# Reordering the opening and the change of sweep of a two-sweep graph kernel, spreading the first rows with TensorE, loading each weight block once, and computing one more product from fp32r words

## The chip, the cores and the metric

The kernel runs on one core of one Trainium2 chip. The metric is the device time of one execution in microseconds, the median of several runs. Repeats of one kernel spread by 1 to 9.5 us, up to 0.34%, and the profiled execution can be any of them, so a difference of a few us between two profiles proves nothing by itself.

## The reference

64 samples, each of 256 tokens with 768 features. Each is layer-normalised and rectified, and three matrices are applied: to the neighbours' mean (`adj`), to the reverse neighbours' mean, and to the token itself. Terms of rank one (biases, degrees, relation embeddings) and the input are added.

```python
h = jnp.maximum(_layernorm(x), 0.0)                       # (64, 256, 768)
ctx = jnp.matmul(adj, h @ Wadj.T + badj) / deg_c[..., None]
ctx = ctx + jnp.matmul(radj, h @ Wrev.T + brev) / rdeg_c[..., None]
ctx = ctx + h @ Wself.T + bself
rel = agg @ Wr.T + br * deg[..., None] + ragg @ Wrr.T + brr * rdeg[..., None]
return x + ctx + rel
```

## The kernel before

For each sample the aggregated features form a left matrix of two token halves (a, b) by three kinds (0, 1, 2). The weights form a right matrix of three kinds by three blocks of 256 columns, so nine blocks of 768 x 256. The kernel replaces 18 block products by 15 products of sums, listed with the right-hand sums they need:

```python
PRODUCTS = {
    6: ("a0+a2+b2", "+01 -20"),
    12: ("a0+a2+b0+b2", "-01"),
    1: ("b0", "-00 +10 +01"),
    # ... (12 more)
}
```

The 15 weight sums are not all held at once: there are two sweeps over the 64 samples. Sweep one makes the left matrices and does eight products, then stores left matrices and partial sums to DRAM. Sweep two reads them back and does the other seven (7, 9, 15, 6, 4, 12, 1).

A product is six matmuls of 128x128 by 128x256. As plain float32 that is 12 records. A product is summed up in a *bank*, an accumulator in PSUM that the listings call x, y, z and so on. Some products are instead made of **words**: both operands are split into a rounded fp32r part and two scaled differences, and three groups of six fp32r matmuls replace the plain ones. The first two groups must come first in their bank, because the bank is then rescaled as a whole (condensed):

```python
def split_left(b, n):
    nc.scalar.activation(first, value, AF.Copy, scale=LOWER)
    top = top_copy(b, n, first.bitcast(F32))              # ScalarE, into the one PSUM tile "top"
    nc.vector.tensor_tensor(others, value, top, op=ALU.subtract)
    nc.vector.scalar_tensor_tensor(diff, others, -STEP, top, op0=ALU.mult, op1=ALU.add)

def product_first(b, n, bank):                            # 12 word matmuls, start=True, then
    nc.scalar.activation(bank, bank, AF.Copy, scale=1.0 + 1.0 / STEP)

def add_out(b, bank, sign, c, n, many=1):                 # DVE: o (+/-)= bank
```

Everything is scheduled by hand: strings such as `STEP2` name the steps in program order, and each engine works through its own instructions in that order; in the traces below an addition on DVE that was ready at about 1695 us ran at 1707.55, behind three sums that stand before it. A quote mark means "the next sample", a caret a sample of sweep two named while sweep one still runs (`load^` sample 0, `load^^` sample 1), a number alone a product, `W`/`V` loads a weight block, `w`/`v` combines blocks in place, `s` splits a left operand, `5a` is the first part of product 5 in words, `u` aggregates, `o`/`out` load and store partial sums. The change of sweep began by loading left operands from ScalarE's queue (condensed):

```python
def change_sweep():
    first_sweep.close()
    second["pool"] = main.enter_context(tc.tile_pool(name="second", bufs=1))
    load_left(0); load_sums(0, 0, 2); load_left(1)
STEP2 = "7a a0+a2+b0+b2 a1+a2' b1+b2' a0+a2' 9 s4 15a 7 6 load'' s9' 15 4a tokT 12 s7' o0' 4 out0 s15' 9a' a0+a2+b2' 1 out1 o1'"
```

## Time and profile before

| | before |
|---|---|
| median of 3 runs | 2839.2 us |
| TensorE busy | 2736.3 us, 96% |
| period in sweep one / sweep two | 25.53 / 16.60 us a sample |
| last sample of sweep one starts | 1716.67 us |
| TensorE idle, 0 to 250 us | 73 us |

The page gives totals; the busy time by stretch shows where TensorE is not full; the timeline shows starts and lengths of single groups. TensorE's instructions overlap, so lengths are read from start to start. The lines are in the prediction below.

For the bookkeeping I use two markers that exist in all kernels: the start of product 10 of the last sample in sweep one, and the start of product 7 of the last sample in sweep two.

### The profile page before, as it was taken

What the parts mean: (1) busy time and instruction counts of PE and PEld (TensorE: products, weight loads), DVE (VectorE), ACT (ScalarE), POOL (GpSimd) and SP (SyncE); (2) the same over time, 40 slices, a digit from 0 to 9 for tenths busy, and PEclk for the clock granted to TensorE, in tenths of its full rate; (3) what the DMA queues carried; (4) which work ended last, traced back from release to release, by engine and by line L of the source; (5) the groups of instructions that cost most, each with busy time, mean ns of one, the idle gap of its engine ahead of it and who ended that gap; (6) DMA issues with size and microseconds to landing.
All of it is one profiled execution on the core that took longest, in us unless ns stands there. A gap on an engine that the chain in (4) does not pass through costs nothing.

```text
span 2837.7 us, 43467 instructions
## 1 busy us (share of the span) xinstructions
PE 2736.3 (96%) x16112; PEld 2488.7 (88%) x16112; DVE 1817.8 (64%) x2892; ACT 1498.4 (53%) x2734; POOL 1864.6 (66%) x1289
## 2 busy tenths in 40 slices
PE   4789999999999999999999997999999999999999
PEld 3578988898888888888888986899999999999998
DVE  4566666666666666666666664666666666666665
ACT  3356565655666565655666552444444444444443
POOL 4477777777777777777777775555555555555553
PEclk8899999999999999999999998999999999999999
DMA  8367777777777777777777767566666666666664
GB/s 268 130 231 264 251 260 272 258 257 257 262 270 257 253 259 273 258 258 254 262 271 257 252 239 270 196 251 236 238 246 247 232 240 252 238 237 244 251 236 159
DMA packets 240353, 698.48 MB, mean 246 GB/s; under 512 B 19444, under 2 KB 100852, under 8 KB 223752
## 3 DMA queue, kind: packets, MB, share of 16 engines
q1 hardware_dynamic: 203272, 393.64, 40.9%
q10 hardware_dynamic: 36864, 302.01, 28.1%
q8 instruction: 129, 2.11, 0.3%
q14 instruction: 88, 0.72, 0.1%
HBM read 439.46 MB, written 256.11 MB: 245 GB/s over the span
## 4 chain that ended last, share of the span: by engine, by line
PE 93%; DVE 3%; DMA 2%; ACT 1%; issue 0%; POOL 0%; ACTq 0%; SPq 0%; DVEq 0%; POOLq 0%
PE y L530 19%; PE x L530 19%; PE pa L496 12%; PE z L530 7%; PE w L530 7%; PE u L519 3%; PE v L519 3%; PE t L519 3%; PE x L519 3%; PE w L519 3%; PE y L519 3%; PE z L519 3%; PE u L530 2%; PE v L530 2%; PE t L530 2%; DVE w L258 1%
## 5 line engine op out<-in xcount | busy, mean ns | idle before, releaser
L513 POOL TENSOR_TENSOR X<-X,Xs 128x768 f32<-128x768 f32 x256 | 472.1, 1866 | 493.7 <-DVE l L293 217.8
L530 PE MATMUL y<-w,X 128*128 128x256 f32 x2304 | 536.4, 383 | 18.9 <-POOL X L513 9.2
L530 PEld LDWEIGHTS y<-w,X 128*128 128x128 f32 x2304 | 432.2, 192 | 80.1 <-POOL X L513 9.5
L485 POOL TENSOR_TENSOR xT<-xT,row 128x1536 f32<-128x1536 f32 (+1 forms) x128 | 447.3, 3494 | 70.9 <-DMA row<-d 65.9
L496 PE MATMUL pa<-a,hilo 128*128 128x512 f32 x1536 | 416.1, 399 | 33.5 <-DVE hilo L452 18.2
L501 DVE TENSOR_TENSOR X<-pa,row 128x512 f32<-128x512 f32 x384 | 264.0, 689 | 183.5 <-PE pa L496 175.4
L530 PE MATMUL x<-w,X 128*128 128x256 f32 x1548 | 356.8, 380 | 8.0 <-DVE o L543 8.0
L277 ACT ACTIVATE top<-l 128x768 f32<-128x768 f32 x350 | 285.3, 815 | 145.9 <-DVE l L294 47.3
L496 PEld LDWEIGHTS pa<-a,hilo 128*128 128x128 f32 x1536 | 271.0, 191 | 80.6 <-DVE hilo L452 22.8
L294 DVE SCALAR_TENSOR_TENSOR l<-l,top 128x768 fp32r<-128x768 f32 x350 | 333.8, 954 | 12.0
L530 PEld LDWEIGHTS x<-w,X 128*128 128x128 f32 x1548 | 285.6, 191 | 42.7 <-issue 8.3
L513 POOL TENSOR_TENSOR b2-a<-Xs,X 128x768 f32<-128x768 f32 x64 | 116.0, 1812 | 196.2 <-ACT hilo L446 162.4
L452 DVE SCALAR_TENSOR_TENSOR hilo<-x,cols,top_h 128x768 fp32r<-128x768 f32 x128 | 129.9, 1015 | 163.6 <-ACT top_h L277 163.6
L293 DVE TENSOR_TENSOR l<-X,top 128x768 fp32r<-128x768 f32 x186 | 176.5, 949 | 11.8 <-ACT top L277 11.4
L530 PE MATMUL z<-w,Xs 128*128 128x256 f32 x768 | 177.9, 382 | 0.0
L530 PE MATMUL w<-w,a1+b 128*128 128x256 f32 x768 | 176.4, 379 | 0.0
L530 PE MATMUL x<-w,Xs 128*128 128x256 f32 x768 | 176.2, 379 | 0.0
L291 ACT ACTIVATE l<-X 128x768 fp32r<-128x768 f32 x186 | 155.6, 836 | 22.4 <-issue 19.9
L530 PEld LDWEIGHTS z<-w,Xs 128*128 128x128 f32 x768 | 142.7, 192 | 18.9
L530 PEld LDWEIGHTS w<-w,a1+b 128*128 128x128 f32 x768 | 141.3, 190 | 18.6
L530 PEld LDWEIGHTS x<-w,Xs 128*128 128x128 f32 x768 | 141.0, 190 | 17.1 <-DVE o L543 0.4
L545 DVE TENSOR_TENSOR o<-o,y 128x256 f32<-128x256 f32 x128 | 53.5, 418 | 156.7 <-PE y L535 156.7
(182 smaller groups left out, 5567.9 us busy)
## 6 DMA issues: line engine op xcount, KB each, us to landing
kept_X<-X ACTq DMA_DIRECT2D x64, 1536.0 KB
X<-kept_X ACTq DMA_DIRECT2D x64, 1536.0 KB
o<-in_x_dram SPq DMA_DIRECT2D x128, 384.0 KB
xT<-in_x_t_dram SPq DMA_DIRECT2D x64, 768.0 KB
kept_Xs<-Xs ACTq DMA_DIRECT2D x64, 768.0 KB
sums<-o SPq DMA_DIRECT2D x128, 384.0 KB
Xs<-kept_Xs ACTq DMA_DIRECT2D x64, 768.0 KB
o<-sums SPq DMA_DIRECT2D x128, 384.0 KB
```

The source lines that it names most:

```text
L277: nc.scalar.activation(top.rearrange("p (f i) -> p f i", i=of.shape[-1]), of, AF.Copy)
L291: nc.scalar.activation(first, value, AF.Copy, scale=LOWER)
L293: nc.vector.tensor_tensor(others, value, top, op=ALU.subtract)
L294: nc.vector.scalar_tensor_tensor(diff, others.bitcast(F32), -STEP, top, op0=ALU.mult, op1=ALU.add)
L452: nc.vector.scalar_tensor_tensor(hilo[:, 1, c, :], S[b]["x"][:, c, :], rstd, top, op0=ALU.mult, op1=ALU.subtract)
L485: eng.tensor_tensor(v, v, row[:, k : k + 1, :].to_broadcast([P, f1 - f0, L]), op=op)
L496: nc.tensor.matmul(pa, hilo[:, part, c, ts(f, P)], s["a"][:, c, :, :].rearrange("p s i -> p (s i)"), start=(k == 0), stop=(k == 2 * C - 1),)
L501: nc.vector.tensor_mul(s["X"][:, f, :, :].rearrange("p s i -> p (s i)"), pa, s["row"][:, 2:4, :].rearrange("p s i -> p (s i)"))
L513: (eng or nc.gpsimd).tensor_tensor(L[name], L[x], L[y], op=op)
L519: nc.tensor.matmul(bank, l[k][:, f, :], r[k][:, f, :], start=(k == 0 and f == 0), stop=(k == 1 and f == F - 1))
L530: nc.tensor.matmul(bank, l[:, f, :], r[:, f, :], start=(start and f == 0), stop=(row is None and f == F - 1), skip_group_check=not start,)
L545: nc.vector.tensor_sub(o, o, bank)
```

## The change

The intent was to fill TensorE's holes in the opening and between the sweeps, and to take some of its cycles away in sweep two. The core of the diff, with cuts marked:

```diff
-    "12": (12, "x", 4, ((-1, 1, 1),)),
-    "1": (1, "x", 5, ((-1, 1, 0),)),
+    "12": (12, "x", 4, ((-1, 1, 0, 2),)),
+    "1a": (1, "s", None, None),
+    "1": (1, "s", 5, ((-1, 1, 0),)),
 ...
 FIRST = """
-o0 o1 adj xt W10 degrees0 degrees1 statistics0 statistics1 tokens spread adj' x' W"11" W5 rows1 ...
+o1 o0 statistics0 adj degrees0 statistics1 xt degrees1 x' W10 tokens W02 left normalise0 normalise1
+statistics0' W12 spread row1 row0 W20 adj' second1 rows1 W11 degrees0' second0 self0 u5 u4 self1 u3 u0 W22 ...
 SECOND = """
-o1' 10a left' self0' self1' degrees0'' degrees1'' u0' 5a 10 statistics0'' statistics1'' tokens'' u1' 5 8 ...
+u2' 5a x'' b2-a1 degrees0'' o0 o1' degrees1'' a1+b1 b0+b1 u5' self0' self1' u3' 10a a1+b0+b1 a0+a1+b0+b1 5
+statistics0'' 10 statistics1'' u1' 8 11a tokens'' 11 ...
 LAST1 = """
-10a sweep2 5a 10 5 V7 V9 V15 s11 V6 V4 V12 flag a0+a2^ a1+a2^ ... v1 out0
+sweep2 10a a0+a1+b0+b1 10 a2+b2 5a V11 5 flag V21 8 load^ v15 s11 14 13 V20 V00 11a v4 V01 11 V10 o0^ b1+b2^
+2 a1+a2^ load^^ a0+a2^ v6 out0 v1 V22 3 out1 a0+a2+b2^ v9 v7 v12
 FIRST2 = """
+o1 a0+a2' 9 6 s9' load'' a0+a2+b0+b2 a1+a2' 4 tokT 7 12 1 out0 a1+a2'' o0' 15 o1' s7' 9a' out1 a0+a2''
 STEP2 = """
+b1+b2' 7a 9 s4 15a a1+a2' a0+a2' a0+a2+b2' 7 load'' s1 4a 15 a0+a2+b0+b2 6 tokT s9' o0' 1a 4 s7' 12 out0 o1'
+1 s15' out1 9a'
-IN_WORDS = {5: 2, 10: 3, 11: 4, 9: 1, 7: 1, 15: 2, 4: 2}
+IN_WORDS = {5: 2, 10: 3, 11: 4, 9: 1, 7: 1, 15: 2, 4: 2, 1: 2}
 ...
+        def row_first(k):                                  # rows of sample 0: broadcast by 4 matmuls with the identity
+                    nc.tensor.matmul(pb[...], col.to_broadcast([P, P]), ident, start=True, stop=True)
+            nc.scalar.activation(S[0]["row"][:, 2 * k : 2 * k + 2, :]..., pb, AF.Copy)
 ...
         def change_sweep():
-            load_left(0)
-            load_sums(0, 0, 2)
-            load_left(1)
```

For sample 0 the rectification also moves from ScalarE to DVE and the top copies of its normalised features fall away. Each of the nine weight blocks is loaded once per sweep at most (nine loads for twelve in sweep one, seven for eight in sweep two), and the sums are made from them.

More of the change, by code (lines that the diff above doesn't have):

```diff
@@ L90 @@
     "4": (4, "t", None, ((-1, 0, 1), (1, 1, 1))),
-    "12": (12, "x", 4, ((-1, 1, 1),)),
-    "1": (1, "x", 5, ((-1, 1, 0),)),
+    "12": (12, "x", 4, ((-1, 1, 0, 2),)),
+    "1a": (1, "s", None, None),
+    "1": (1, "s", 5, ((-1, 1, 0),)),
 }
 FIRST = """
-o0 o1 adj xt W10 degrees0 degrees1 statistics0 statistics1 tokens spread adj' x' W"11" W5 rows1
-W8 W11 W"22" normalise0 normalise1 second0 second1 degrees0' degrees1' adj'' left self0 self1 relu
-u0 u1 u2 u3 u4 u5 W14 W2 W"01" W3 W13 W"20" statistics0' statistics1' tokens' rows2 xt' store
@@ L100 @@
-b2-a1 b0+b1* a1+b1 a1+b0+b1 w10
-o1' 10a 5a 10 5 w8 turn14 normalise0' normalise1' 8 w11 spread' rows3 a0+a1+b0+b1 11a 14 w2 11
-a2+b2 second0' second1' x'' w3 left' self0' self1' degrees0'' degrees1'' u0' statistics0'' statistics1'' tokens''
-2 3 w13 u1' out1 o0' relu' u2' u3' adj''' xt'' spread'' 13 u4' u5' store' normalise0'' normalise1'' second0'' b2-a1' b0+b1' second1'' x'''
-a1+b1' a1+b0+b1' out0
+o1 o0 statistics0 adj degrees0 statistics1 xt degrees1 x' W10 tokens W02 left normalise0 normalise1
@@ new lines @@
+statistics0' W12 spread row1 row0 W20 adj' second1 rows1 W11 degrees0' second0 self0 u5 u4 self1 u3 u0 W22
+w8 u2 u1 statistics1' degrees1' W21 a1+b1 W00 b0+b1* storeX relu W01 w3 xt' tokens' rows2 b2-a1 spread'
+normalise0' w11 a1+b0+b1 a0+a1+b0+b1 w5 storeXs normalise1' second1' adj'' w13 5 11 second0' x'' rows3
+self0' w14 left' w2 u2' 8 3 w10 u4' o1' degrees0'' 14 self1' statistics0'' degrees1'' adj''' a2+b2
+statistics1'' 10 u0' u5' u3' relu' out1 tokens'' u1' xt'' spread'' normalise0'' second0'' storeXs' 13
@@ L105 @@
+normalise1'' second1'' 2 storeX' left'' out0
 """
 SECOND = """
-o1' 10a left' self0' self1' degrees0'' degrees1'' u0' 5a 10 statistics0'' statistics1'' tokens'' u1' 5 8
-relu' u2' u3' a0+a1+b0+b1 11a 14 a2+b2 adj''' 11 u4' xt'' 2 spread'' u5' 3 normalise0'' normalise1''
-out1 o0' 13 store' second0'' b2-a1' b0+b1' second1'' x''' s10' s5' a1+b1' a1+b0+b1' out0
+u2' 5a x'' b2-a1 degrees0'' o0 o1' degrees1'' a1+b1 b0+b1 u5' self0' self1' u3' 10a a1+b0+b1 a0+a1+b0+b1 5
+statistics0'' 10 statistics1'' u1' 8 11a tokens'' 11 relu' u0' xt'' adj''' u4' normalise1'' spread'' a2+b2 3
@@ L110 @@
+b2-a1' storeX' normalise0'' b0+b1' second1'' 14 second0'' 2 s10' x''' s5' a1+b1' 13 storeXs' out1 o0' out0
+a1+b0+b1'
 """
 STEP1 = """
-left' degrees0'' u1' self0' 10a u2' 5a statistics0'' self1' u0' 5 statistics1'' 10 s11 degrees1'' adj''' o1' u3' relu' 8 11a u4' tokens'' u5' a0+a1+b0+b1 xt'' 11 normalise1'' b2-a1' spread'' store' second1'' a2+b2 14 b0+b1' s10' 3 normalise0'' second0'' a1+b1' 2 13 x''' out0 a1+b0+b1' out1 o0' s5'
+left' degrees0'' u1' self0' 10a u2' 5a statistics0'' self1' u0' 5 statistics1'' 10 s11 degrees1'' adj''' o1' u3' relu' 8 11a u4' tokens'' u5' a0+a1+b0+b1 xt'' 11 normalise1'' b2-a1' spread'' storeX' storeXs' second1'' a2+b2 14 b0+b1' s10' 3 normalise0'' second0'' a1+b1' 2 13 x''' out0 a1+b0+b1' out1 o0' s5'
@@ L113 @@
 """
 LAST1 = """
-10a sweep2 5a 10 5 V7 V9 V15 s11 V6 V4 V12 flag a0+a2^ a1+a2^ a0+a2+b2^ b1+b2^ a0+a1+b0+b1 8 V1 a2+b2 11a 14 11 V"10" v6 2 v4 3 turn12 out1 13 v1 out0
+sweep2 10a a0+a1+b0+b1 10 a2+b2 5a V11 5 flag V21 8 load^ v15 s11 14 13 V20 V00 11a v4 V01 11 V10 o0^ b1+b2^
+2 a1+a2^ load^^ a0+a2^ v6 out0 v1 V22 3 out1 a0+a2+b2^ v9 v7 v12
 """
 FIRST2 = """
-o1 o0' load'' tokT 9 a0+a2+b0+b2 a0+a2' a1+a2' a0+a2+b2' b1+b2' 15 7 6 s9' 4 s7' 12 out0 o1' s15' 9a' 1 out1
+o1 a0+a2' 9 6 s9' load'' a0+a2+b0+b2 a1+a2' 4 tokT 7 12 1 out0 a1+a2'' o0' 15 o1' s7' 9a' out1 a0+a2''
@@ L119 @@
+"""
+SECOND2 = """
+a0+a2+b2 tokT 4 b1+b2 7a 9 s9' 15 6 9a' 7 load'' o0' out0 a0+a2+b0+b2 s7' o1' b1+b2' 12 s15' 1 out1
+a0+a2+b2' s15
 """
 STEP2 = """
-7a a0+a2+b0+b2 a1+a2' b1+b2' a0+a2' 9 s4 15a 7 6 load'' s9' 15 4a tokT 12 s7' o0' 4 out0 s15' 9a' a0+a2+b2' 1 out1 o1'
+b1+b2' 7a 9 s4 15a a1+a2' a0+a2' a0+a2+b2' 7 load'' s1 4a 15 a0+a2+b0+b2 6 tokT s9' o0' 1a 4 s7' 12 out0 o1'
+1 s15' out1 9a'
 """
@@ L126 @@
     5: (0, 12, 13), 10: (1, 8, 9), 8: (2,), 11: (3, 10, 11), 14: (4,), 3: (5,), 13: (6,), 2: (7,),
-    "22": (8,), "11": (9,), "20": (10,), "01": (11,),
+    "10": (0,), "02": (4,), "12": (3,), "00": (6,), "21": (7,), "22": (8,), "11": (9,), "20": (10,), "01": (11,),
 }
 PLACES2 = {
-    7: (8, 3, 4), 9: (9, 10, 11), 15: (1, 7, 5), 6: (12,), 4: (13, 6, 14), 12: (0,), 1: (2,),
-    "10": (3,),
+    7: (8, 3, 4), 9: (9, 10, 11), 15: (1, 7, 5), 6: (12,), 4: (13, 6, 14), 12: (0,), 1: (2, 15, 16),
+    "22": (8,), "20": (9,), "11": (1,), "21": (13,), "01": (0,), "00": (2,), "10": (3,),
 }
-IN_WORDS = {5: 2, 10: 3, 11: 4, 9: 1, 7: 1, 15: 2, 4: 2}
+IN_WORDS = {5: 2, 10: 3, 11: 4, 9: 1, 7: 1, 15: 2, 4: 2, 1: 2}
 @with_exitstack
@@ L225, in place @@
         def place(i, dtype, name):
-            pool = second["pool"] if i == 14 else pool1
+            pool = second["pool"] if i >= 14 else pool1
             return pool.tile([P, F, NB], dtype, tag=f"w{i}", name=name)
-        def load_weights(places, which):
-            for n in which:
-                right = PRODUCTS[n][1] if n in PRODUCTS else "+" + n
-                k, o = int(right[1]), int(right[2])
-                W[n] = place(places[n][0], F32, f"w{n}")
-                v = (wadj_t, wrev_t, wself_t)[k].rearrange("(f p) o -> p f o", p=P)
-                nc.sync.dma_start(W[n], v[:, :, ts(o, NB)])
-                if len(right) == 3:
-                    W[right[1:]] = W[n]
@@ L240, in turn, with load_block @@
-        def turn(n):
-            nc.scalar.activation(W[n], W[n], AF.Copy, scale=-1.0)
-            W["-" + PRODUCTS[n][1][1:]] = W.pop(PRODUCTS[n][1][1:])
-        def combine_weights(n, eng):
-            first, *others = PRODUCTS[n][1].split()
-            sign = first[0]
-            for other in others:
-                m = W.get(other[1:])
-                same = other[0] == "+"
-                if m is None:
-                    m, same = W["-" + other[1:]], not same
-                if same and sign == "-":
-                    eng.tensor_tensor(W[n], m, W[n], op=ALU.subtract)
-                else:
-                    assert sign == "+"
-                    eng.tensor_tensor(W[n], W[n], m, op=ALU.add if same else ALU.subtract)
-                sign = "+"
+        def load_block(places, name):
+            W[name] = place(places[name][0], F32, f"w{name}")
+            v = (wadj_t, wrev_t, wself_t)[int(name[0])].rearrange("(f p) o -> p f o", p=P)
+            nc.sync.dma_start(W[name], v[:, :, ts(int(name[1]), NB)])
@@ new lines, in combine_weights @@
+        def combine_weights(places, n, eng):
+            at = places[n][0]
+            sign = {term[1:]: term[0] for term in PRODUCTS[n][1].split()}
+            own = [m for m in sign if places[m][0] == at]
+            if own and len(sign) == 1:
+                W[n] = W[own[0]]
+                if sign[own[0]] == "-":
+                    nc.scalar.activation(W[n], W[n], AF.Copy, scale=-1.0)
+                return
+            value = W[own[0]] if own else None
+            minus = own and sign[own[0]] == "-"
+            for m in sorted(sign, key=lambda m: sign[m]):
+                if m in own:
+                    continue
+                if value is None:
+                    value = W[m]
+                    continue
+                if own or n in W:
+                    to = value
+                else:
+                    to = W[n] = place(at, F32, f"w{n}")
+                if minus:
+                    assert sign[m] == "+"
+                    eng.tensor_tensor(to, W[m], value, op=ALU.subtract)
+                else:
+                    eng.tensor_tensor(to, value, W[m], op=ALU.add if sign[m] == "+" else ALU.subtract)
+                minus, value = False, to
+            W[n] = value
@@ L425, in spread @@
             nc.scalar.activation(line, pt, AF.Copy)
-            d = dram.tile([4, C, P], F32, tag="d", name=f"d_{b}")
-            for c in range(C):
-                nc.sync.dma_start(d[:, c, :], line[c * 64 + NMEAN : c * 64 + RRDEG + 1, :])
             s["row"] = first1.tile([P, 4, L], F32, tag="row", name=f"row_{b}")
-            nc.sync.dma_start(
-                s["row"].rearrange("p k i -> p (k i)"), d.rearrange("k c p -> (k c p)").partition_broadcast(P)
-            )
+            if b > 0:
+                d = dram.tile([4, C, P], F32, tag="d", name=f"d_{b}")
+                for c in range(C):
+                    nc.sync.dma_start(d[:, c, :], line[c * 64 + NMEAN : c * 64 + RRDEG + 1, :])
+                nc.sync.dma_start(
+                    s["row"].rearrange("p k i -> p (k i)"), d.rearrange("k c p -> (k c p)").partition_broadcast(P)
+                )
             s["tokT"] = pool3.tile([P, P], F32R, tag="tokT", name=f"tokT_{b}")
@@ L436, in spread @@
             nc.sync.dma_start(s["line"], line)
+        def row_first(k):
+            pb = ps2.tile([P, 512], F32, tag="pa", name=f"pb{k}")
+            for m in range(2):
+                for c in range(C):
+                    col = cols[0][:, c, NMEAN + 2 * k + m : NMEAN + 2 * k + m + 1]
+                    nc.tensor.matmul(
+                        pb[:, m * L + c * P : m * L + (c + 1) * P], col.to_broadcast([P, P]), ident, start=True, stop=True
+                    )
+            nc.scalar.activation(S[0]["row"][:, 2 * k : 2 * k + 2, :].rearrange("p k i -> p (k i)"), pb, AF.Copy)
         def normalise(b, c):
@@ L444, in normalise @@
             hx = s["x"][:, c, :]
-            nc.scalar.activation(hx, s["o", c] if b == 0 else hx, AF.Relu, bias=v[:, c, NMEAN : NMEAN + 1])
+            if b == 0:
+                nc.vector.tensor_scalar(hx, s["o", c], v[:, c, NMEAN : NMEAN + 1], 0.0, op0=ALU.add, op1=ALU.max)
+            else:
+                nc.scalar.activation(hx, hx, AF.Relu, bias=v[:, c, NMEAN : NMEAN + 1])
             nc.scalar.activation(hilo[:, 0, c, :], hx, AF.Copy, scale=v[:, c, RSTD : RSTD + 1])
@@ L450, in second_half @@
             rstd = cols[b % 2][:, c, RSTD : RSTD + 1]
-            top = top_copy(b, f"h{c}", hilo[:, 0, c, :].bitcast(F32).unsqueeze(1))
+            first = hilo[:, 0, c, :].bitcast(F32)
+            top = first if b == 0 else top_copy(b, f"h{c}", first.unsqueeze(1))
             nc.vector.scalar_tensor_tensor(
@@ L462, in new_left, with store_left @@
             s["L"] |= {f"{'ab'[c]}2": s["Xs"][:, :, ts(c, P)] for c in range(C)}
-        def store_left(b):
+        def store_left(b, n):
+            many = 2 if n == "X" else 1
             s = S[b]
-            for n, many in (("X", 2), ("Xs", 1)):
-                s["kept_" + n] = kept.tile([P, F, many, L], F32, name=f"kept_{n}_{b}")
-                nc.scalar.dma_start(s["kept_" + n], s[n] if many > 1 else s[n].unsqueeze(2))
+            s["kept_" + n] = kept.tile([P, F, many, L], F32, name=f"kept_{n}_{b}")
+            nc.scalar.dma_start(s["kept_" + n], s[n] if many > 1 else s[n].unsqueeze(2))
         def load_left(b):
@@ L590, in main_path @@
             "adj": load_adj, "x": load_x, "xt": load_xt, "tokens": token_values, "spread": spread,
-            "left": lambda b: new_left(b, 1), "relu": relu_features, "store": store_left,
+            "left": lambda b: new_left(b, 1), "relu": relu_features,
+            "storeX": lambda b: store_left(b, "X"), "storeXs": lambda b: store_left(b, "Xs"),
             "load": load_left, "tokT": tok_rows,
@@ L595, in main_path @@
             "degrees": degrees, "statistics": statistics, "normalise": normalise, "second": second_half,
-            "self": self_features, "u": aggregate,
+            "self": self_features, "u": aggregate, "row": lambda b, k: row_first(k),
         }
@@ L601, in run @@
             for item in order.split():
-                name = item.rstrip("'")
-                b = M + len(item) - len(name)
+                name = item.rstrip("'^")
+                b, in_sweep = M + len(item) - len(name), sweep
+                if item[-1] == "^":
+                    b, in_sweep = len(item) - len(name) - 1, 2
                 stem, digit = name[:-1], name[-1]
@@ L607, in run @@
                 elif name[0] in "WV":
-                    which = name[1:].strip('"')
-                    load_weights(PLACES1 if name[0] == "W" else PLACES2, (which if '"' in name else int(which),))
+                    load_block(PLACES1 if name[0] == "W" else PLACES2, name[1:])
                 elif name[0] in "wv":
-                    combine_weights(int(name[1:]), nc.vector)
-                elif name.startswith("turn"):
-                    turn(int(name[4:]))
-                elif name[-1] == "^":
-                    combine_left(0, stem)
+                    combine_weights(
+                        PLACES1 if name[0] == "w" else PLACES2, int(name[1:].rstrip("*")),
+                        nc.gpsimd if name[-1] == "*" else nc.vector,
+                    )
                 elif b >= B:
@@ L627, in run @@
                 elif name in ("o0", "o1"):
-                    load_sums(b, int(digit), sweep)
+                    load_sums(b, int(digit), in_sweep)
                 elif name in ("out0", "out1"):
@@ L647, in main_path @@
         for t in range(B):
-            run(STEP2 if t > 0 else FIRST2, t, 2, PARTS2, PLACES2)
+            run(FIRST2 if t == 0 else SECOND2 if t == 1 else STEP2, t, 2, PARTS2, PLACES2)
     def general_path(sub: ExitStack):
```

## The prediction

> **What bounds the kernel now.** I read the totals of the page first, then the busy time by stretch, then the timeline of TensorE in one steady sample, then the waits of the two places where TensorE stands still. The page's totals:
>
> ```profile
> PE 2736.3 (96%) x16112; PEld 2488.7 (88%) x16112; DVE 1817.8 (64%) x2892; ACT 1498.4 (53%) x2734; POOL 1864.6 (66%) x1289
> ```
>
> TensorE is the bound; the others have a third or more in hand. The busy time by stretch shows where TensorE is not full (columns: stretch, its length, busy time of each engine, granted clock, DMA share, GB/s):
>
> ```profile
> 0.00:25.00 25.00, 5.74 (x11) 3.14 (x12) 9.74 (x19) 13.47 (x35) 8.43 (x16) 1.00 0.75 251
> 25.00:50.00 25.00, 16.45 (x48) 11.89 (x46) 11.44 (x17) 0.72 (x4) 10.71 (x12) 0.80 0.90 308
> 50.00:75.00 25.00, 10.31 (x39) 8.26 (x39) 11.95 (x8) 11.90 (x15) 14.57 (x5) 0.78 0.62 201
> 75.00:100.00 25.00, 17.07 (x58) 13.29 (x59) 17.36 (x22) 5.28 (x16) 2.50 (x8) 0.74 0.33 116
> 100.00:150.00 50.00, 38.01 (x152) 30.05 (x150) 21.02 (x33) 20.32 (x38) 28.41 (x20) 0.86 0.50 184
> ...
> 400.00:1600.00 1200.00, 1200.00 (x6725) 1078.64 (x6724) 792.07 (x1365) 725.92 (x1410) 925.74 (x706) 1.00 0.73 261
> ...
> 1700.00:1750.00 50.00, 37.90 (x195) 33.55 (x194) 17.35 (x27) 6.38 (x11) 19.96 (x12) 0.83 0.78 284
> 1750.00:1800.00 50.00, 40.41 (x201) 35.12 (x200) 33.43 (x35) 19.07 (x20) 34.41 (x14) 0.93 0.51 179
> ...
> 2000.00:2700.00 700.00, 700.00 (x4638) 660.35 (x4637) 460.65 (x677) 334.72 (x548) 385.29 (x213) 1.00 0.68 241
> ```
>
> Both steady stretches are solid TensorE. The holes are the opening (idle 19.3+8.6+14.7+7.9+12.0 = 62 us of the first 150, 10 more to 250, at clocks of 0.74 to 0.86) and the change of sweep (12.1+9.6 us, clocks 0.83 and 0.93). So three things can pay: fewer TensorE cycles in sweep two, a denser opening, a denser change. In sweep two, TensorE's timeline (start, length, engine, line, output<-inputs, count):
>
> ```profile
> 2107.30 2.75 PE L530 MATMUL x<-w,Xs 128*128 128x256 f32 x12
> 2109.70 1.06 PE L530 MATMUL u<-w,l 128*128 128x256 f32 x6
> 2110.60 0.88 PE L519 MATMUL t<-w,t 128*128 128x256 f32 x6
> 2111.31 0.88 PE L519 MATMUL t<-w_others,t 128*128 128x256 f32 x6
> 2112.03 2.75 PE L530 MATMUL x<-w,X 128*128 128x256 f32 x12
> 2114.43 0.47 PE L535 MATMUL x<-rows,tokT 128*128 128x256 f32 x1
> 2114.74 0.87 PE L530 MATMUL t<-w,t 128*128 128x256 f32 x6
> ...
> 2116.88 2.75 PE L530 MATMUL x<-w,X 128*128 128x256 f32 x12
> ...
> 2133.48 2.75 PE L530 MATMUL x<-w,X 128*128 128x256 f32 x12
> ```
>
> Ends overlap, so go by starts. A plain product (12 records) holds TensorE 2112.03 to 2114.43 = 2.40 us; six word matmuls hold it 0.72, so a product in words (18) costs 2.15. What follows a plain product is 0.18-0.19 late: 0.90 instead of 0.72 at 2109.70, 0.31 for the row. The line at 2116.88 is product 1; its next is 16.60 later. Check: 3 plain x 2.40 + 12 word groups x 0.717 + 2 rows x 0.12 + 3 switches x 0.18 = 16.58.
>
> At the change of sweep the waits name the cause:
>
> ```profile
> ACT y L522 <- DMA o<-sums: 10.9, 1, 10.9
> ...
> PE y L530 <- ACT y L522: 9.5, 1, 9.5
> ...
> PE x L530 <- DVE o L543: 8.0, 1, 8.0
> ```
>
> ScalarE issues the loads of kept left operands for samples 0 and 1 and stands in that queue; behind it waits the rescaling of bank y, and behind that TensorE. The second hole, 7.95 us at 1766, is DVE busy combining and splitting late weight blocks.
>
> **What the Trainium skill says.** "TensorE: Matmul & The Clock Gate", Part 1 (the HAM clock gate): after an idle window of about 3.4 us the array runs at half clock until it has been busy about as long. The trace agrees: after the hole of 9.2 us at 64.27 a product's records take 4.44 us instead of 2.75, and after the 2.6 us at 1734 they take 5.49. A hole thus costs more than its length. "GPSIMD Engine Reference", 1. Specifications: GpSimd shares its SBUF interfaces with VectorE when that reads two SBUF inputs. The trace agrees: a weight combination of 1.75 us took 3.35 at 38.44, and GpSimd's additions of 1.8 took 2.51 and 3.20 beside it. "DMA: Bandwidth & Descriptors", Anatomy of one DMA: a DMA has about 2.0 us of fixed cost, mostly the write receipt. The trace agrees roughly: the first rows leave at 12.54, go through DRAM in two dependent transfers, and release GpSimd at 18.03, 5.5 us.
>
> **Product 1 in words.** Removed for samples 2 to 63: a plain product, 2.40, and its switch, 0.18. Added: 18 word matmuls, 2.15. In the new order TensorE has two plain products (6 and 12) and two switches: 2 x 2.40 + 2 x 0.18 + 15 x 0.717 + 0.24 = 16.16. Gain 0.44 us a sample, x 62 = **27 us**. Added elsewhere per sample: ScalarE one copy (0.83), one top copy (0.81), one rescale (0.37); DVE 0.95+0.95, and product 12's subtraction widened from 256 to 512 columns (0.42 to 0.68). DVE goes from 10.9 (461/700 x 16.6) to about 13.0 of 16.16, 80%; ScalarE from 7.9 to 9.9. Neither becomes the bound by volume. The own bank is the fourth of a pool of four that had three users.
>
> **Opening.** Removed: three of twelve weight blocks (0.79 MB each; at the 350 GB/s the queue shows when busy, 2.2 us each, 6.7 in all), the DRAM trip of the first rows (an eight-matmul broadcast and two copies instead, row about 2 us earlier), two ScalarE passes of 0.92, moved to DVE, and two top copies of 0.8. The weights also come sooner: in the old order the last blocks are issued at 45 to 52 us, in the new I put the last landing at about 40. Walking the new order by each engine's row durations, I get the first aggregation at 17, the first product at about 35 (was 41.9), little idling afterwards, and the end of the first order near 70, where the old one finishes its last aggregation at 101. Against it: DVE is nearly full from 12 to 50 us, and combinations of sample 1 (four GpSimd additions, 7.3 us) move from the first order to the second, together with the 7.1 us of self features. That is 31 us earlier. I take some off for contention and for the additions pushed into the second order, and put some back because with fewer holes the clock stays up until 250 us: **33 us**, 10 to 48.
>
> **Change of sweep.** The loads now stand behind product 8, product 2 and single blocks, one block fewer is read, and the combinations come later. The 9.5 us hole and its cold start (about 5 us) should vanish; the 8 us hole should shrink, though sample 1 now splits three weight blocks instead of two (each ties up DVE and ScalarE some 6.8 us in turn). Lost now: 23 idle, 6 cold = about 30 us. I take **17 us**, 5 to 25.
>
> Sum: 2839.2 - 27 - 33 - 17 = 2762.
>
> **Rivals.** *First, the split chain becomes the bound of sweep two.* There is one top tile: copy (0.81), subtraction (0.95), second difference (0.95) must finish before the next copy. With releases that is about 2.9 us, and five of them make 14.5 of 16.16, with some 3.5 us of DVE additions to fit between; the profile already shows ScalarE waiting 2.15 us for it. For it: little slack. Against it: my walk through one period puts product 4's operand 0.4 us before its deadline, the others 1 us or more. If it bound, sweep two would stay at 16.6 or worse: gain 0 or below, total near 2790 or higher. *Second, the opening is bound by DMA or DVE whatever the order,* so that the reordering only moves idle time: 12 MB stand before the last weight block, and the queue already ran at 350 GB/s from 45 to 60. Opening gain then under 10, total about 2786. *Third, the catch-up hides it:* after the opening TensorE is the bound, nothing refills a hole, so a gain there stays; I give this no weight. *Fourth, at the change the 12 MB of left operands, weights and sums set the pace* (36 us at 350 GB/s against 53 us of TensorE work): the left operands of sample 0 would still come late and about half of the 30 us stay lost, total 2764 to 2770.
>
> **Range and chances.** The 27 us are firm within 5 unless the chain binds (one in eight). Opening and change have about 15 and 8 us of error. 80% range 2735 to 2795. Two per cent is 2782.4; the sweep-two gain alone (1%) does not reach it, with half of the rest it does: 0.84 faster, 0.15 within, 0.01 slower.
>
> **What would show it.** Right: product 1 as 18 records of 0.12 us in bank s, a period of 16.1 to 16.2 us, TensorE 100% from 1850 on; TensorE busy in the first 150 us up from 88 to about 115; no gap over 5 us after the last sample of sweep one starts. Wrong: TensorE waiting on DVE l or ScalarE top in the steady part of sweep two; gaps before products behind DVE weight combinations at 35 to 100 us; the left operands of sample 0 landing after sample 63's products have ended.

## The result

The changed kernel takes **2764.7 us** in the median (2763.4 to 2767.1, 4 runs) against 2839.45 in the same rounds. The ratio is 0.9739, 95% interval 0.9722 to 0.9756. Here and below a ratio is the mean time of one kernel's runs over that of the other's in the same rounds, so it is not quite the quotient of the medians.

The page's totals of the changed kernel:

```profile
PE 2698.8 (98%) x16500; PEld 2474.2 (90%) x16500; DVE 1963.7 (71%) x3020; ACT 1619.1 (59%) x2920; POOL 1876.4 (68%) x1289
```

TensorE has only 37.5 us less busy time while the span is 75.2 us shorter: half of the gain is idle time of TensorE that is gone. The busy time by stretch of the changed kernel (columns as before):

```profile
0.00:25.00 25.00, 10.66 (x38) 8.17 (x39) 15.67 (x27) 9.21 (x31) 9.30 (x16) 0.93 0.91 303
25.00:50.00 25.00, 12.95 (x46) 8.79 (x45) 24.14 (x22) 10.86 (x19) 19.27 (x14) 0.93 0.92 324
50.00:75.00 25.00, 23.66 (x99) 18.72 (x99) 17.89 (x23) 15.60 (x32) 23.21 (x15) 0.94 0.53 180
75.00:100.00 25.00, 23.91 (x111) 20.23 (x110) 14.88 (x24) 13.00 (x22) 23.28 (x16) 1.00 0.74 277
100.00:150.00 50.00, 48.30 (x249) 42.18 (x248) 32.03 (x51) 21.93 (x43) 36.53 (x28) 1.00 0.62 222
...
1650.00:1700.00 50.00, 41.73 (x222) 35.91 (x220) 20.35 (x29) 7.30 (x11) 26.62 (x14) 0.98 0.76 279
1700.00:1750.00 50.00, 36.92 (x175) 32.20 (x176) 36.42 (x36) 23.71 (x25) 22.07 (x9) 0.85 0.50 175
...
1850.00:2700.00 850.00, 850.00 (x6108) 817.53 (x6107) 687.38 (x946) 519.43 (x840) 483.17 (x265) 1.00 0.68 247
```

The opening is dense from 50 us on and the clock stays up. Between 25 and 50 us DVE is the full engine (24.14 of 25). The change of sweep, now at 1667 to 1756, is as full of holes as it was. Sweep two is solid TensorE, with DVE at 81% and ScalarE at 61%.

TensorE's timeline in sweep two, two samples of the changed kernel:

```profile
2101.67 2.75 PE L559 MATMUL x<-w,Xs 128*128 128x256 f32 x12
2104.07 1.05 PE L548 MATMUL s<-w,l 128*128 128x256 f32 x6
2104.96 0.89 PE L548 MATMUL s<-w_others,l 128*128 128x256 f32 x6
...
2109.11 0.87 PE L559 MATMUL s<-w,l 128*128 128x256 f32 x6
...
2117.84 2.75 PE L559 MATMUL x<-w,Xs 128*128 128x256 f32 x12
```

Bank s holds product 1 in three word groups. Product 6 comes again after 16.17 us.

With the two markers, the spans of the profiles divide without a rest:

| part | before | after | gained |
|---|---|---|---|
| opening: start of the last sample of sweep one | 1716.67 | 1667.18 | 49.5 |
| sweep two: 61 times the steady period (samples 2 to 63) | 61 x 16.60 | 61 x 16.17 | 26.2 |
| change of sweep: what lies between | 87.5 | 88.6 | -1.1 |
| tail after product 7 of the last sample starts | 20.9 | 20.4 | 0.5 |
| span | 2837.7 | 2762.5 | 75.2 |

(The third row is the start of product 7 of the last sample, 2816.79 and 2742.12, less 61 periods, less the first row; so what sample 2 takes above the steady period counts as change of sweep.) The total is near the predicted one, but the parts are not: the opening gained half as much again as predicted, and the change of sweep, which was to give 17, gave nothing. The hole that took the place of the old ones, first in TensorE's timeline around the change of sweep:

```profile
1692.42 2.75 PE L559 MATMUL x<-w,X 128*128 128x256 f32 x12
1708.06 4.77 PE L559 MATMUL x<-w,Xs 128*128 128x256 f32 x12 [12.89 <-issue]
```

The first is product 9 of sample 0, the second product 6, which adds into the same bank x. After the wait product 6 also runs slowly, 4.77 us for 2.75: this is called a cold start here. The profile names nothing for the wait of 12.89 us. The timeline of the other engines in the same stretch does:

```profile
1697.33 8.35 POOL L542 TENSOR_TENSOR X<-X,Xs 128x768 f32<-128x768 f32 x3 [4.56 <-DMA Xs<-kept_Xs]
1697.46 3.28 DVE L269 TENSOR_TENSOR w<-w,w 128x1536 f32<-128x1536 f32 x1 [7.58 <-DMA w<-in_Wadj_dram]
1700.67 3.35 DVE L267 TENSOR_TENSOR w<-w,w 128x1536 f32<-128x1536 f32 x1
1704.06 3.24 DVE L269 TENSOR_TENSOR w<-w,w 128x1536 f32<-128x1536 f32 x1
...
1707.55 0.41 DVE L572 TENSOR_TENSOR o<-o,x 128x256 f32<-128x256 f32 x1
```

DVE must read product 9 out of bank x (1707.55) before product 6 may add into it. In DVE's program order the sums for products 6 and 1 come first, and these wait until 1697.46 for one weight block. (The first of the three is product 6's own weight sum, ready at 1700.74, so only the rest of the hole, about 7 us, is a matter of DVE's order.) They then take 3.3 us each instead of 1.75, because GpSimd adds at the same time: its three additions take 8.35 us instead of about 5.4. The Trainium skill, "SBUF — State Buffer", SBUF: two separate sides, says that the port pair shared by the two engines is an exclusive lock for a whole instruction. The trace agrees nearly: 3 x 1.75 + 3 x 1.82 = 10.7 us of work one after the other, done in 10.0, which is 0.7 less than a strict lock would allow.

### The profile page after: what moved, and what is told of

Same layout as the page of the kernel before. It is cut to its first block, busy times and chain, and to the rows that moved or that the text cites.

```text
span 2762.5 us, 44550 instructions
## 1 busy us (share of the span) xinstructions
PE 2698.8 (98%) x16500; PEld 2474.2 (90%) x16500; DVE 1963.7 (71%) x3020; ACT 1619.1 (59%) x2920; POOL 1876.4 (68%) x1289
## 4 chain that ended last, share of the span: by engine, by line
PE 94%; DMA 2%; DVE 1%; POOL 1%; ACT 1%; issue 1%; SPq 0%; ACTq 0%; POOLq 0%; DVEq 0%
PE y L559 19%; PE x L559 14%; PE pa L525 13%; PE w L559 8%; PE z L559 8%; PE t L548 3%; PE y L548 3%; PE x L548 3%; PE s L548 3%; PE u L548 3%; PE v L548 3%; PE z L548 3%; PE w L548 3%; PE s L559 2%; PE t L559 2%; PE u L559 2%
## 5 line engine op out<-in xcount | busy, mean ns | idle before, releaser
L542 POOL TENSOR_TENSOR X<-X,Xs 128x768 f32<-128x768 f32 x256 | 478.7, 1891 | 468.4 <-DMA Xs<-kept_Xs 451.5
L289 ACT ACTIVATE top<-l 128x768 f32<-128x768 f32 x391 | 319.0, 816 | 147.4 <-DVE t L306 46.7
L306 DVE SCALAR_TENSOR_TENSOR l<-l,top 128x768 fp32r<-128x768 f32 x391 | 373.0, 954 | 13.5
L305 DVE TENSOR_TENSOR l<-X,top 128x768 fp32r<-128x768 f32 x227 | 215.7, 950 | 35.3 <-ACT top L289 35.1
L303 ACT ACTIVATE l<-X 128x768 fp32r<-128x768 f32 x227 | 189.9, 837 | 24.4 <-issue 22.2
L559 PE MATMUL x<-w,Xs 128*128 128x256 f32 x768 | 178.2, 382 | 14.4 <-issue 12.9
L559 PE MATMUL x<-w,X 128*128 128x256 f32 x780 | 180.3, 381 | 3.5 <-DVE o L572 3.5
L559 PEld LDWEIGHTS x<-w,X 128*128 128x128 f32 x780 | 144.2, 191 | 20.9 <-issue 3.7
```

The lines of the kernel that those rows point to most:

```text
L289: nc.scalar.activation(top.rearrange("p (f i) -> p f i", i=of.shape[-1]), of, AF.Copy)
L306: nc.vector.scalar_tensor_tensor(diff, others.bitcast(F32), -STEP, top, op0=ALU.mult, op1=ALU.add)
L542: (eng or nc.gpsimd).tensor_tensor(L[name], L[x], L[y], op=op)
L559: nc.tensor.matmul(bank, l[:, f, :], r[:, f, :], start=(start and f == 0), stop=(row is None and f == F - 1), skip_group_check=not start,)
```

## The experiments

Twelve kernels ran, all correct. The first three undo one part of the change each.

**Product 1 left plain.**

```diff
-IN_WORDS = {5: 2, 10: 3, 11: 4, 9: 1, 7: 1, 15: 2, 4: 2, 1: 2}
+IN_WORDS = {5: 2, 10: 3, 11: 4, 9: 1, 7: 1, 15: 2, 4: 2, 1: 99}
```

> The changed kernel with product 1 left plain (own bank and new orders kept). Theory: the words alone are worth 0.43 us a sample (period 16.17 after, 16.60 before), so the period goes back to 16.60 and the time to 2764.7 + 62 x 0.43 = 2791. Rival: the new orders or the own bank carry part of it, then the period stays below 16.5 and the time below 2785; or the words cost something elsewhere, then above 2795.

Measured: 2800.2 us (2793.7 to 2802.3), ratio 0.9863. The period is 16.71, not 16.60: with product 1 plain, product 12 stands behind a single word group (product 4) that itself follows a plain product, and its 12 records take 2.48 us from start to start instead of 2.40. So neither line of the expectation held exactly. In the new order the words are worth 0.54 us a sample, 33 us in all, of which 0.11 a sample only repairs what the new order costs a plain product. Against the kernel before they are worth 0.43. This kernel has no third block of weights to split at sample 1. By the markers its change of sweep takes 84.4 us, 4.2 less than the changed kernel's, and the period after product 7 of sample 2 is 16.71 where the changed kernel has 19.76. The profiled execution is the fastest of the four (2793.7), so the 4.2 is an indication of what the third split costs and not a firm number.

**The opening of before** (both orders, twelve loads, rows through DRAM, rectification and top copies on ScalarE).

```diff
+FIRST, SECOND, PLACES1 and the functions for loading and combining weights in sweep one: as before
-            if b > 0:                                     # in spread
+            if b >= 0:
+            nc.scalar.activation(hx, s["o", c] if b == 0 else hx, AF.Relu, bias=...)
```

> The changed kernel with the opening of before (first and second order, twelve weight loads, first rows through DRAM, relu and top copies on ScalarE). Theory from the two traces: the opening carries 49.5 us, so the first product of the last sample in sweep one starts again near 1716 and the time is about 2814. Rival (my prediction): the opening is worth 33, then about 2798, the rest of the 49.5 would have to come from elsewhere.

Measured: 2815.0 us, ratio 0.9911; the last sample of sweep one starts at 1717.07. The opening is worth 50 us, as the traces said, not 33.

**The change of sweep of before.**

```diff
+LAST1, FIRST2 and the weight loads of sweep two: as before; STEP2 used for sample 1
+            load_left(0); load_sums(0, 0, 2); load_left(1)   # in change_sweep
```

> The changed kernel with the change of sweep of before (order of the last sample and of sample 0, eight weight loads, loads of left operands at the start). Theory from the two traces: the new change of sweep gained nothing (about -1 us), so 2762 to 2767. Rival (my prediction): it is worth 17, then about 2782.

Measured: 2772.7 us (2772.2 to 2773.1), ratio 0.9764. Undoing the new change of sweep costs 6 to 8 us, so both lines missed: it did gain something. By the markers this kernel's change of sweep takes 94.0 us, 6.5 more than that of the kernel before and 5.4 more than the new one. The likely source of the 6.5 is product 1 in words, whose weights are a third block to split at sample 1; the orders of the steady samples differ too, so this is argued. The run with product 1 plain, above, points the same way with 4.2. In this kernel TensorE waits there in three places; two are shown (the third, 7.60 us at 1726.67, is the 7.95 of the kernel before):

```profile
1684.12 1.65 PE L590 MATMUL y<-w,l 128*128 128x256 f32 x6 [10.32 <-ACT y L582]
...
1763.53 1.65 PE L590 MATMUL x<-w,t 128*128 128x256 f32 x6 [6.67 <-ACT x L582]
```

The first is the old hole behind ScalarE's queue. The second, 6.67 us, was 1.59 us in the kernel before. In front of it stand the splits of three weight blocks, in the kernel before of two. The new order closed the first hole and the 7.60, opened one of 12.9 us and one of 3.54, and carried the third split.

**One split more in sweep two.** A rival of the prediction was that the chain of splits through the one top tile would become the bound. This kernel does one split twice, with the same result.

```diff
+            if n == 1:                                    # in split_left, the same four instructions again
+                nc.scalar.activation(first, value, AF.Copy, scale=LOWER)
+                top = top_copy(b, "again", first.bitcast(F32))...
+                nc.vector.tensor_tensor(others, value, top, op=ALU.subtract)
+                nc.vector.scalar_tensor_tensor(diff, others, -STEP, top, op0=ALU.mult, op1=ALU.add)
```

> The changed kernel with the split of product 1's left operand done twice in sweep two (same tiles, same result): one more pass of first copy, top copy and two differences a sample. Theory of the split chain (one top tile, 2.9 us a split, 6 x 2.9 = 17.4 over the period of 16.17): the period becomes 17.4 or more, the time 2840 or more. Rival (volume): DVE has 13.1 of 16.17 us busy, one more split makes 15.0, which still fits, so the time stays within 5 us of 2765.

Measured: 2849.0 us, ratio 1.0034. In the timeline of TensorE product 7 starts every 17.45 us in most periods (after the first ones a few take up to 18.4). Product 1's second word group in bank s waits for DVE's split, 0.6 us in the mean of the 40 waits from 2000 to 2700 us. Two starts of product 7:

```profile
2806.93 0.88 PE L553 MATMUL v<-w,l 128*128 128x256 f32 x6
...
2824.38 0.88 PE L553 MATMUL v<-w,t 128*128 128x256 f32 x6
```

```profile
1850.00:2700.00 850.00, 808.33 (x5617) 759.54 (x5617) 722.69 (x971) 551.82 (x875) 439.65 (x242) 1.00 0.65 230
```

17.45 / 6 = 2.91 us a split, the 2.9 that the prediction had added up. DVE is only 85% busy and ScalarE 65% (second fence, the busy time by stretch), so it is the chain through one tile that binds, not the volume of either engine. In the changed kernel five splits take about 14.5 of 16.17 us: this rival was close, and one more product in words would lose.

**Rows of the first sample through DRAM again.**

```diff
-            if b > 0:
+            if b >= 0:
-... spread row1 row0 W20 ...
+... spread W20 ...
```

> The changed kernel with the first rows sent through DRAM again (eight broadcast matmuls and two copies taken out), all else kept. Theory: the rows were about 5.5 us in DRAM in the old kernel and land about 2 to 5 us later than the broadcast; DVE is full from 12 to 50 us, so the wait goes through to the end: first product 3 to 5 us later, time 2767 to 2770. Rival: the opening waits for weight blocks or for DVE's later work, then the delay is absorbed, under 1 us. Neither gives the whole 50 us of the opening.

Measured: 2767.3 us (2765.6 to 2769.5), ratio 0.9737; the changed kernel has 0.9739 and 0.9743. The first product starts 3.9 us later (38.8 for 34.8), as the theory says, but the runs show no loss beyond their spread. The profiled run happened to be the slowest, and its last sample of sweep one is 7 to 8 us late; the other runs of this kernel do not bear out so much. So this part is worth 0 to 3 us, and how much of that is open.

**The first order new, the second order old.**

```diff
-FIRST = ... storeX' left'' out0
+FIRST = ... storeX' b2-a1' b0+b1' x''' a1+b1' a1+b0+b1' out0
+SECOND = "o0 " + the second order of before
```

> The changed kernel with its new first order but the second order of before (the four additions and the load that the old first order had at its end put back there). In the traces 29 us of the 50 were gained by the end of the first order, 21 in and after the second. Theory: the second order itself carries these 21, so the last sample of sweep one starts about 18 to 21 us later and the time is about 2783 to 2786. Rival: the first order hands over a better state (samples further ahead, warm clock) and the old second order would do as well: within 7 us of 2765.

Measured: 2786.0 us (2782.8 to 2792.3), ratio 0.9801: about 20 of the opening's 50 us go when the second order goes (18 by the ratios, 21 by the medians). TensorE's timeline and that of the others around the new hole:

```profile
92.47 5.45 PE L558 MATMUL y<-w,X 128*128 128x256 f32 x12 [10.78 <-DVE o L571]
```

```profile
82.33 6.92 POOL L513 TENSOR_TENSOR xT<-xT,row 128x1536 f32<-128x1536 f32 x2
...
91.25 0.18 DVE L425 RECIPROCAL cols<-cols 128x4 f32<-128x4 f32 x1 [6.53 <-POOL cols L424]
...
91.92 0.41 DVE L571 TENSOR_TENSOR o<-o,y 128x256 f32<-128x256 f32 x1
```

In the old second order the reciprocal of the next sample's degrees stands before product 5's addition on DVE. It waits for small GpSimd operations, which stand behind GpSimd's self features of 6.9 us. TensorE's product 8 waits for bank y all that time and then starts cold (5.45 us for 2.75). The new second order puts the additions of products 5 and 10 ahead of that reciprocal. It is the same pattern as in the change of sweep: a bank that is not freed because its addition stands behind something unrelated in DVE's order.

**Three weight blocks more in the opening.**

```diff
+                    more = place(12, F32, "more")         # after W02, W20 and W22; nothing reads it
+                    nc.sync.dma_start(more, wself_t...[:, :, ts(0, NB)])
```

> The changed kernel with three more weight blocks of 0.79 MB read in the opening, at the places of the queue where the old order had its repeats; nothing reads them. Theory of my prediction: the queue is the opening's limit for the weights, so three blocks cost 6.7 us (2.2 each), 2771. Rival from the trace of the changed kernel: DVE has 24.1 of 25 us busy from 25 to 50 us and waits for no weight block there, so the loads are hidden: under 2 us, 2764 to 2767.

Measured: 2768.5 us (2766.2 to 2772.5), ratio 0.9754 against 0.9743 of the control (2766.6), intervals overlapping: 2 to 3 us more, between the two expectations. It was run on another chip. The trace shows that the loads are not hidden. DVE now does wait for weight blocks (1.08, 2.58 and 1.42 us), its busy time from 25 to 50 us falls from 24.14 to 19.66, and TensorE waits behind it:

```profile
39.48 2.88 DVE L267 TENSOR_TENSOR w<-w,w 128x1536 f32<-128x1536 f32 x1 [2.58 <-DMA w<-in_Wself_dram]
```

```profile
45.68 4.74 PE L559 MATMUL w<-w,X 128*128 128x256 f32 x12 [6.68 <-DVE w L269]
```

This product starts at 41.22 in the changed kernel. The end of the first order is 3.8 us late (76.6 for 72.8) and the last sample of sweep one 3.2 us against the control's profile, 3.9 against the changed kernel's. So loading each block once is worth about 2 to 4 us of the 6.7 that I had put down, not clear of the noise of the times. With nine loads DVE is the full engine; with twelve the queue is close enough to make it wait.

**The control,** the changed kernel itself, unedited:

> The changed kernel itself, as the control of this job. All theories: 2763 to 2767, 0.974 of before.

Measured: 2766.6 us (2762.6 to 2768.4), ratio 0.9743. It was run on another chip.

The last four look for the 13 us hole. **The late block early:**

```diff
-... 5a V11 5 flag V21 8 load^ v15 s11 14 13 V20 V00 11a v4 V01 11 V10 ...
+... 5a V11 5 flag V21 V01 8 load^ v15 s11 14 13 V20 V00 11a v4 11 V10 ...
```

> The changed kernel with one block of weights (the one that products 6, 1 and 12 take) loaded right after product 5 of the last sample in place of after product 11's first part. Theory: the 13 us hole before product 6 of sample 0 comes from this block's landing at 1697: behind it DVE's three combinations hold up product 9's addition and with it bank x. Landing 8 us or so sooner, the hole shrinks to 3 to 7 us and the time to 2756 to 2760. Rival: the DMA queues are full there (10 MB in 26 us), so another block or the left operands become late instead, and the hole stays within 3 us of 13.

Measured: 2766.8 us, ratio 0.974, no gain. TensorE's timeline:

```profile
1692.30 2.86 PE L559 MATMUL w<-w,a1+b 128*128 128x256 f32 x12 [3.78 <-DVE o L574]
1705.73 5.41 PE L559 MATMUL x<-w,Xs 128*128 128x256 f32 x12 [7.86 <-issue]
```

The hole before product 6 shrank by 5 us, but product 3 now waits 3.78 for another addition, behind the sum for product 4, whose block is the late one now. The rival was right about the time and about another block being late (later on DVE also waits 4.68 us for a third one), while the hole itself shrank about as the theory said.

**Product 1's sums late:**

```diff
-2 a1+a2^ load^^ a0+a2^ v6 out0 v1 V22 3 out1 a0+a2+b2^ v9 v7 v12
+2 a1+a2^ load^^ a0+a2^ v6 out0 V22 3 out1 a0+a2+b2^ v9 v7
-o1 a0+a2' 9 6 s9' ...
+o1 a0+a2' 9 6 v1 v12 s9' ...
```

> The changed kernel with product 1's two combinations and product 12's sign change moved behind product 6 of sample 0. Theory: DVE's strict order makes the 13 us hole, so product 6 starts 5 to 7 us sooner; but products 12 and 1 then wait for these combinations, which stand behind the split of product 9's weights, so a new hole of 5 us or more opens there and the time stays within 4 us of 2765. Rival: DVE's order is all of it and the gain of 6 us stays: about 2758.

Measured: 2761.5 us (2758.8 to 2765.2), ratio 0.9723 (0.9707 to 0.9739), some 4 to 5 us faster than the changed kernel, though the intervals still overlap. The timeline:

```profile
1701.67 5.46 PE L559 MATMUL x<-w,Xs 128*128 128x256 f32 x12 [6.18 <-issue]
...
1731.91 4.40 PE L559 MATMUL u<-w,X 128*128 128x256 f32 x12 [4.49 <-POOL X L542]
```

The hole halved, as the theory of DVE's order says. The new hole before product 12 that I expected did not come (0.33 us). Another did, before product 15 of sample 1: its operand stands on GpSimd behind sample 2's sums, which wait for sample 2's load.

**A new change of sweep.**

```diff
-sweep2 10a ... V11 5 flag V21 8 load^ v15 s11 14 13 V20 V00 11a v4 V01 11 V10 o0^ b1+b2^
-2 a1+a2^ load^^ a0+a2^ v6 out0 v1 V22 3 out1 a0+a2+b2^ v9 v7 v12
+sweep2 10a ... V11 5 flag V21 V01 8 load^ v15 s11 14 13 V20 V00 11a 11 V10 V22 o0^ b1+b2^
+2 a1+a2^ a0+a2^ v4 out0 3 out1 a0+a2+b2^ v6 v1 v12 load^^ v9 v7
-o1 a0+a2' 9 6 s9' load'' a0+a2+b0+b2 a1+a2' 4 tokT 7 12 1 out0 a1+a2'' o0' 15 o1' s7' 9a' out1 a0+a2''
+o1 15 9 a0+a2+b0+b2 4 6 a0+a2' s9' load'' a1+a2' tokT 7 12 1 out0 a0+a2+b2' o0' o1' s7' 9a' out1 b1+b2'
-a0+a2+b2 tokT 4 b1+b2 7a 9 ...                           # SECOND2
+a1+a2' tokT 4 a0+a2' 7a 9 ...
```

> The changed kernel with a new change of sweep: products 15, 9 and 4 of sample 0 before product 6, the block for 6 early, the load of sample 1's left operands after the combinations, sample 1's operands on GpSimd ahead of sample 2's. Theory: the 13 us hole is a matter of what waits for what (DVE's order and one block's landing) and three products that need nothing late can fill it: gain 10 to 14 us, 2751 to 2755. Rival: the bytes set the pace (7 blocks and 2 samples of left operands in about 30 us), so the hole moves to sample 1's start: gain under 4 us.

Measured: **2757.6 us** (2756.2 to 2763.8), ratio 0.9712, interval 0.9699 to 0.9725, against 0.9743 (0.9728 to 0.9757) of the control. It was run on another chip. It is the fastest kernel, 0.3% faster than the changed kernel, and lies between the two expectations. The profiled run was this kernel's slowest, so its absolute times say little, but its timeline still shows where the rest of the hole went:

```profile
1708.57 5.46 PE L559 MATMUL x<-w,Xs 128*128 128x256 f32 x12 [6.14 <-DVE o L572]
...
1735.88 5.49 PE L559 MATMUL x<-w,Xs 128*128 128x256 f32 x12 [4.31 <-DVE o L572]
```

In the first, DVE waits 7.96 us for the partial sums of sample 0. Their load was issued at 1699.65, with the 2.36 MB of sample 1's left operands, delayed by me, issued at the same moment. One wait was traded for another once more.

**The same with two weight splits spread over later samples.**

```diff
-IN_WORDS = {..., 15: 2, 4: 2, 1: 2}
+IN_WORDS = {..., 15: 2, 4: 3, 1: 4}
```

> change_b with the weights of products 4 and 1 split one and two samples later (products 4 and 1 plain for one and two samples more). Theory: three splits in one sample (each about 6.8 us of DVE and ScalarE in turn) hold up sample 1 and 2 by 4 to 6 us; spread, they fit beside the steady work, less 0.3 to 0.5 us for each plain product: another 3 to 5 us, 2747 to 2751. Rival: sample 1 is held by the landing of its left operands, so under 1 us.

Measured: 2760.1 us (2757.3 to 2761.4), ratio 0.9717: no gain over the one before. It was run on another chip. The traces show why, from product 7 of one sample to that of the next. From samples 1 and 2 these periods are 23.3 and 21.9 us in the version before and 17.7 and 17.1 here; from samples 3 and 4 they are 16.2 and 16.2 there and 20.3 and 22.4 here. From sample 1 to sample 5 it is 77.5 and 77.4 us. So samples 1 and 2 did get shorter, as the theory said, but the late splits did not fit beside the steady work: the loss moved on by two samples.

## Why the prediction was right, and where its steps failed

*What bounds the kernel.* Right: TensorE is busy throughout the steady periods of both kernels (700 of 700 us before, 850 of 850 after), and what was gained was gained in cycles there or in holes. One reading of the working is wrong: the 5.49 us at 1734 do not follow from the hole of 2.6 us. Before it came the hole of 9.54 us that ends at 1729.97, after which TensorE ran for only 1.65 us; elsewhere a hole of 2.37 us (1736.03 in the last kernel above) left a group at 2.83 us.

*Product 1 in words.* Right: 27 predicted, 26.2 measured over the steady stretch, the period 16.17 for 16.16. DVE at 81% (80 predicted) and ScalarE 9.9 us of each period (9.9) also came out. Of the 0.43, 0.25 are the words as such (2.40 against 2.15) and 0.18 one switch from plain to word matmuls less. What the step left out is the price in the change of sweep of a third block of weights to split, by the markers about 4 us in the new order and 6.5 in the old one. The prediction named that split under the change of sweep, with 6.8 us of DVE and ScalarE, but gave its loss no number of its own.

*Opening.* Under-sized: 33 predicted, 49.5 measured, just beyond the part's own range of 10 to 48. The walk through the first order was good: first product at 35 (34.84), end of the order near 70 (72.8, where the last of product 2 ends; the old one ended at 101.4), so 31 predicted and 28.6 measured. The failing term is the next one, "I take some off ..., and put some back": a net 2 us for everything after the first order, measured at 21. In the traces the way from the end of the first order to the start of the last sample is 1615.3 us before and 1594.4 after. I looked at what the second order would get to do in addition, and not at what the old one made wait; the run with the old second order shows 20 us there. Two terms came to less: blocks loaded once 2 to 4 us for 6.7, rows by TensorE 0 to 3 ("row about 2 us earlier" was 0.24: GpSimd takes it up at 17.79 for 18.03). How the remaining 22 to 26 of the first order divide among order and engines was not taken apart. One of the named signs of being wrong did appear: TensorE waits 3.63 us at 41.22 behind a combination of weights on DVE.

*Change of sweep.* Over-sized: 17 predicted, 5 to 8 measured when it is undone alone, and -1.1 against the kernel before, since the third split, it seems, took back what the order gave (84.4 us without it, 88.6 with it, 87.5 before). The failing step is "The 9.5 us hole and its cold start should vanish; the 8 us hole should shrink". The first did vanish. But I did not walk DVE's order there as I did in the opening, and so missed that product 9's addition stands behind three sums that wait for one weight block, a new hole of 12.9 us and a cold start. The fourth rival, that bytes set the pace, has much for it: from 1675 to 1700 us the queues moved 377 GB/s at a busy share of 1.03, three rearrangements moved the hole from one wait to another, and the best gained 9 us. What it named, sample 0's left operands, was not the load that came late; a weight block was. That the rest could not be gained at all is argued from these three and not shown.

*The sum.* 2762 predicted, 2764.7 measured: an error of +16 in the opening and one of -18 in the change of sweep cancelled. That the total is right is luck; two of its three terms were off by half or more.

*The rivals.* The split chain did not bind, and the extra split shows both that the mechanism was sized correctly (2.91 us a split) and that about 1.6 us a sample were left. The opening bound by DMA or DVE whatever the order is refuted by the 49.5 us themselves (it allowed under 10), though the three extra blocks show the queue not far behind DVE. The expected sign "TensorE busy in the first 150 us up from 88 to about 115" came out at 119.5; "no gap over 5 us after the last sample of sweep one starts" failed.

## What to carry to other kernels

Where every engine runs strictly in program order, a hole on the bounding engine is best walked back through the *order* of the engine that frees its accumulator, not only through the dependencies: twice here an addition that was ready stood behind an unrelated operation that waited for a DMA or for GpSimd. When a part is moved to fill a hole, walk the same stretch for every engine and every load after the move; near a limit in bytes the wait tends to reappear at the next load. A total that agrees does not confirm its parts: two markers in both traces that split the span without a rest are cheap, and undoing each part alone shows what the parts cost each other.

## What the Trainium skill lacked or had wrong

- "TensorE: Matmul & The Clock Gate" does not state what a plain float32 matmul costs beside an fp32r one, and "FP8 and Floating Point Precision", TensorE Precision Notes, says four passes. Here a 128x128 by 128x256 matmul takes 0.400 us plain and 0.1195 in fp32r words, a factor of 3.35.
- No page has the cost of changing from plain to fp32r matmuls: the following group starts 0.18 to 0.19 us late (0.90 us from start to start instead of 0.72), 3 times a sample before the change and 2 after.
- "SBUF — State Buffer" (SBUF: two separate sides) gives the rule of the exclusive lock but no size for two engines that alternate: DVE's sum of 128x1536 takes 3.3 us instead of 1.75 while GpSimd's addition of 128x768 takes 2.8 instead of 1.8.
